# Loading x one pair of steps ahead in a cross-attention kernel

## The chip, the core and the metric

The kernel runs on one core of a Trainium2 chip. The metric is the time of one execution on the device in microseconds (us), given as the median of several runs. The core has five engines with queues of their own, each executed in order: TensorE (PE, with its weight loads shown as PEld), VectorE (DVE), ScalarE (ACT), GpSimd (POOL) and SyncE (SP). Here SP issues every DMA. Engines wait for each other, and for DMAs, by semaphores.

## What is computed

Cross-attention with 8 heads of width 256, a residual and a layer norm, in float32. x is 16 x 256 x 256, the context is 16 x 77 x 192, the mask 16 x 77.

```
Q, K, V = x @ Wq, context @ Wk, context @ Wv        (per head)
attn = softmax(where(mask, Q K^T / sqrt(256), -inf))
out = (attn V) @ Wo + x
result = (out - mean) * rsqrt(var + 1e-5) * gamma + beta
```

## The kernel before

**Folded weights.** The first part, up to about 43 us, multiplies weights with each other: gA and gB hold Wk times Wq per head, uA and uB hold Wv times Wo. From then on a batch needs only: `a`, its context with gA and gB (`prepare_a`); scores, x against `a` (`scores`, L289); a softmax; `vw`, its context with uA and uB (`prepare_vw`); and softmax weights times `vw`, which is the attention output before the residual.

**Tiles.** A batch is 256 rows of x, two tiles t of 128 rows (QT = 2, NT = 32 in all). Four batches make a group g (GB = 4, GT = 8 tiles). Each group has two copies of x in SBUF. `xg` has the rows as they are, for the residual; it is loaded by `load_x`, and the output is made in place in it. `xT` is x in transposed blocks, for the scores; `load_xT` (L144) loads it with four DMAs of 128 KB for two batches, one for each quarter of the partitions, and `transpose_x` (L154) turns the 32 x 32 blocks in place, two VectorE instructions for two batches (a pair). The xT of groups 0 and 2 share a buffer, and so do those of groups 1 and 3.

**The loop.** A step b runs from -1 to 14 (L937). In step b the scores of batch b+1 are made and its softmax follows, the product of batch b is made, and batch b-1 is normalised. For b below 13 (NS) the product of a batch is `seven(b)` (L434), seven block products in place of eight. It takes as weights the turned softmax `pT` and four sums of them, `ss`, which GpSimd makes in `sums(b)` (L415 to L418) in the step before. Its seven results are put together by `add_seven(b)`: two adds on VectorE (`add_product`, L483), two adds into m and three adds into `xg` on GpSimd (L469). The last batches use `attend` (L367) in its place.

The steps with odd b, up to b = 9, are long: TensorE also prepares two batches' `vw` and `a` there. The even ones are short. From b = 11 on (`alone`), each step prepares for one batch.

**Order within a step** (the order of the calls is the order on every queue: the schedule is written by hand). VectorE: shifts of the scores (L306, with the mask's `bias`), what the step before left in `behind`, statistics and `rden`, one `normalise` (L533, L552), two turns of softmax weights (L355), then `turn_x_and_normalise`, then `add_seven`'s adds. GpSimd: the softmax weights p (L345), `differences` (L398), then `sums` before `add_seven` in the odd steps up to 9, and `add_seven` before `sums` in the others. After `normalise` of the second tile of a pair, SP stores both (L560). `behind` holds the even steps' second `normalise`; it runs in the next step after the shifts, and so its store stands on SP ahead of that odd step's loads.

**Loads of x.** Group 0: xT in the first queue of loads, x by `load_x(0)` at L854. The other groups, in each odd step: x and xT for two batches that lie b+5 and b+6.

```python
        g, n = (b + 1) // GB + 1, (b + 1) % GB
        if g < NG and n % 2 == 0:
            load_x(g, n, 2 * QT)
            load_xT(g, n * QT, (n + 2) * QT)
```

They are turned one odd step later (batches b+3 and b+4), in `turn_x_and_normalise`, and their scores come in the steps b+2 and b+3.

**Masks.** `load_bias(lo, hi)` broadcasts the masks of some batches to all partitions; `bias_of(lo, hi)` makes them into what the shift adds (L569 to L574). Both are called for batches 0 to 3 and for 4 to 15; the later part is loaded at the end of the first queue of loads and made in step -1.

Of the kernel before, what the change touches and what calls it, by code (L numbers as in the profile page):

```python
# [10 lines left out]
I32 = mybir.dt.int32  # L11
# [5 lines left out]
P = 128  # L17
# [3 lines left out]
GB = 4  # L21
# [6 lines left out]
def kernel(  # L28
# [13 lines left out]
    nc = tc.nc  # L42
    B, S, DI = x.shape
    S2, DL = c.shape[1], c.shape[2]
    LB = DL - P
    CR = 112
    NG = B // GB
    QT = S // P
    NT = B * QT
    GT = GB * QT  # L50
# [48 lines left out]
    bias_f = bias.rearrange("p b k -> p (b k)")  # L99
# [14 lines left out]
    def load_x(g, n=None, of=QT):  # L114
        if not n:
            xg_of[g] = const.tile([P, GT, DI], F32, tag=f"xg{g}", name=f"xg_{g}")
        lo, hi = (0, GT) if n is None else (n * QT, n * QT + of)
        nc.sync.dma_start(xg_of[g][:, lo:hi], x_rows[:, g * GT + lo : g * GT + hi, :])
# [3 lines left out]
    def evacuate(dst, src):  # L122
# [3 lines left out]
        else:  # L126
            nc.vector.tensor_copy(dst, src)


    pools = {}  # L130
    xT_of, a_of, vw_of, p_of, mv_of = {}, {}, {}, {}, {}

    def in_two(name, shape, g):
        return pools[g % 2].tile(shape, F32, tag=f"{name}{g % 2}", name=f"{name}_{g}", bufs=1)

    def load_xT(g, lo=0, hi=GT):


        if lo == 0:
            xT_of[g] = in_two("xT", [P, GT * NM, 2, BK], g)  # L140
        rows = x.rearrange("b s d -> (b s) d")[(g * GT + lo) * P : (g * GT + hi) * P, :]
        rows = rows.rearrange("(m r) (i n) -> i r m n", r=BK, i=NM)
        for i in range(NM):
            nc.sync.dma_start(  # L144
                xT_of[g][i * BK : (i + 1) * BK, lo * NM : hi * NM].rearrange(
                    "p m n q -> p m (n q)"
                ),
                rows[i],
            )

    def transpose_x(g, j):

        cols = xT_of[g][:, j * NM : (j + 2) * NM]
        nc.vector.transpose(cols, cols)  # L154
# [127 lines left out]
    def scores(t):  # L282
        g = t // GT
        j, bl = t % GT, (t // QT) % GB
        ps = [ps_mm.tile([P, 512], F32, tag="mm", name=f"ps_{t}_{a}") for a in range(2)]
        for m in range(NM):
            for dc in range(2):
                for i in range(NM):
                    nc.tensor.matmul(  # L289
                        ps[m // 2][i * BK : (i + 1) * BK, m % 2 * 2 * S2 : (m % 2 + 1) * 2 * S2],  # L290
                        xT_of[g][:, j * NM + m, dc],
                        flat(a_of[g][:, dc, bl, 2 * i : 2 * i + 2, :]),
                        start=(dc == 0),
                        stop=(dc == 1),
                    )
        ps_of[t] = ps
# [234 lines left out]
    def centre(t):  # L531
        y = xg_of[t // GT][:, t % GT, :]
        nc.vector.scalar_tensor_tensor(  # L533
            y, y, mv_of[t // GT][:, t % GT, 0:1], gam, ALU.subtract, ALU.mult
        )

    def store(t):
        nc.sync.dma_start(out_rows[:, t, :], xg_of[t // GT][:, t % GT, :])

    def normalise(t, aside=False, centred=False):  # L540

        g, j = t // GT, t % GT
        rstd, less = rstd_of.pop(t)
        y = xg_of[g][:, j, :]
        if aside:
            nc.scalar.activation(y, y, AF.Identity, bias=less, scale=rstd)
            nc.gpsimd.tensor_tensor(y, y, gam, ALU.mult)
            nc.gpsimd.tensor_tensor(y, y, bet, ALU.add)
        else:
            if not centred:  # L550
                centre(t)
            nc.vector.scalar_tensor_tensor(y, y, rstd, bet, ALU.mult, ALU.add)  # L552
        if t >= NT - 5 * QT:
            store(t)
            return
        done.append(t)
        if t ^ 1 in done:
            t |= 1
            j |= 1
            nc.sync.dma_start(  # L560
                out_rows[:, t + 1 - QT : t + 1, :], xg_of[g][:, j + 1 - QT : j + 1, :]
            )
# [15 lines left out]
    with tc.tile_pool(name="wonce", bufs=1) as wp:  # L578
# [59 lines left out]
            load_blocks(wvT[:, a], wv_blocks[a])  # L638
        for a in range(NF):
            nc.sync.dma_start(wo_of[a // 2][:, a % 2], wo_rows[a])  # L640
        mask_row = mask.rearrange("b k -> (b k)")

        def load_bias(lo, hi):
            nc.sync.dma_start(
                bias_f[:, lo * S2 : hi * S2].bitcast(I32),
                mask_row[lo * S2 : hi * S2].partition_broadcast(P),
            )

        load_xT(0, 0, GT // 2)
        load_bias(0, GB)  # L650
        load_rest()
        load_xT(0, GT // 2, GT)
        load_bias(GB, B)


        idle = ps_mm.tile([P, P], F32, tag="mm", name="idle")
# [169 lines left out]
        def a_of_pairs(*pairs):  # L826
            part_A, part_B, copies = prepare_a(0, pairs)
            part_A()
            part_B()
            for dst, src in copies():  # L830
                nc.scalar.copy(dst, src)
# [19 lines left out]
        for i in range(3):  # L851
            turn_v(i)
        a_of_pairs(2, 3)
        load_x(0)  # L854
        nc.sync.dma_start(gam, gamma.partition_broadcast(P))
        nc.sync.dma_start(bet, beta.partition_broadcast(P))
        turn_v(3)
# [66 lines left out]

    behind = []

    def turn_x_and_normalise(g, n, old):
        to_turn = (g, 0) if g < NG and n == 2 else (g - 1, GT // 2) if g > 1 and n == 0 else None
        if to_turn:
            for j in range(to_turn[1], to_turn[1] + GT // 2, 2):  # L930
                transpose_x(to_turn[0], j)
        if old:
            normalise(old[1])

    assert QT == 2
    last = NT - 1
    for b in range(-1, B - 1):  # L937
        old = range(max(b - 1, 0) * QT, b * QT)
        now = range(max(b, 0) * QT, (b + 1) * QT)
        new = range((b + 1) * QT, (b + 2) * QT)  # L940
        for t in new if b >= 0 else ():
            scores(t)
        if b == B - 2:
            for t in old:
                finish(t)
            spread(old[0], old[-1] + 1)
            invert(old[0], old[-1] + 1, aside=old)
            for t in old:
                normalise(t, aside=True)
        for t in new if b >= 0 else ():  # L950
            shift(t)
        while behind:
            behind.pop(0)()
        g, n = (b + 1) // GB + 1, (b + 1) % GB
        if g < NG and n % 2 == 0:
            load_x(g, n, 2 * QT)
            load_xT(g, n * QT, (n + 2) * QT)
        for m in range(0, 2) if b < 0 else range(b + 2, min(b + 3, B // 2)):
            turn_last(m)
        alone = b + 1 >= B - GB  # L960
        works = work_of(b + 1) if alone or n % 2 == 0 else []
        for part_A, _, _ in works:
            part_A()
        for _, part_B, _ in works:
            part_B()
        for i, t in enumerate(new if b >= 0 else ()):
            exponential(t)
            if old and b < B - 2:
                finish(old[i])
            weigh(t)  # L970
        ahead = works and not alone
        if old and b < B - 2 and not ahead:
            spread(old[0], old[-1] + 1)
        if ahead:
            copy_out(works)
            if old:
                spread(old[0], old[-1] + 1)
            works = work_of(b + 2, rest_first=True)
            for _, part_B, _ in works:
                part_B()  # L980
            for part_A, _, _ in works:
                part_A()
        copy_out(works)
        if b + 1 < NS:
            differences(b + 1)
        if b < NS:
            if now:
                seven(b)
            if old:
                invert(old[0], old[-1] + 1)  # L990
                normalise(old[0])
            for t in new:
                turn(t)
            if b < 0:
                for j in range(GT // 2, GT, 2):
                    transpose_x(0, j)
                bias_of(GB, B)
            if alone or ahead:
                turn_x_and_normalise(g, n, old)
            else:  # L1000
                behind.append(partial(turn_x_and_normalise, g, n, old))
            if ahead:
                sums(b + 1)
            if now:
                add_seven(b)
            if b + 1 < NS and not ahead:
                sums(b + 1)
            continue
        for t in now:
            attend(t)  # L1010
        if b < B - 2:
            invert(old[0], old[-1] + 1, aside=old[:1])
            normalise(old[0], aside=True)
            turn(new[0])
            normalise(old[1])
            turn(new[1])
            for t in now:
                add_product(t)
        else:
            turn(new[0])  # L1020
            finish(now[0])
            spread(now[0], now[1])
            turn(new[1])
# [57 lines left out]
```

## Time and profile before

| | |
|---|---|
| median of 3 runs | 272.82 us (272.69 to 273.63) |
| the profiled execution | 272.17 us |
| its span in the profile | 270.3 us |
| TensorE busy | 263.6 us, 98% of the span |
| GpSimd busy | 171.4 us, 63% |
| VectorE busy | 185.6 us, 69% |
| ScalarE busy | 155.6 us, 58% |
| DMA | 22.69 MB, mean 84 GB/s |
| start of step 3 / 5 / 7 / 9 / 11 / 12 on TensorE (first scores) | 104.94 / 132.82 / 160.70 / 188.58 / 213.42 / 226.01 us |

Times in views are microseconds from the span's start. In a timeline a row is: start, length, engine, line, operation, output<-input, count, and in brackets how long the engine stood idle before it and what ended this. "The chain" is the work that ended last, followed back from the last instruction, at each step to what released it. Instructions of an engine can overlap a little, so a row's end can lie behind the next row's start.

### The profile page before, as it was taken

The page shows a single profiled execution, that of the slowest core. Times are in us where ns is not written, and L with a number is a line of the kernel's source. Part 1 is how long each engine was busy: PE and PEld are TensorE (multiplying, and loading weights), DVE is VectorE, ACT ScalarE, POOL GpSimd, SP SyncE. Part 2 cuts the span into 40 slices and gives each one's busy share as a digit, 9 for nine tenths or more (in the row PEclk, how much of TensorE's full clock was granted, in tenths as well). Part 3 has the DMA queues.
Part 4 walks back from the last instruction along what each step waited for, and adds up shares of the span by engine and source line. Part 5 has one row for each costly group of instructions (what it writes and reads, how often), then busy time and mean ns, then how long its engine had stood idle before and what let it go on. Part 6 is the DMA issues. An engine that isn't in the chain of part 4 may idle for free.

```text
span 270.3 us, 14362 instructions
## 1 busy us (share of the span) xinstructions
PE 263.6 (98%) x6104; PEld 190.5 (70%) x6104; DVE 185.6 (69%) x808; ACT 155.6 (58%) x652; POOL 171.4 (63%) x231
## 2 busy tenths in 40 slices
PE   7999999999999999999999999999999999999993
PEld 6557588754894599449954996489769969684662
DVE  0555938583464858863796479646977898988765
ACT  3233325835858555964687377729584592945752
POOL 1000005726389757996699759964999798966654
PEclk9999999999999999999999999999999999999999
DMA  6998999993000010261016100910091010110102
GB/s 194 203 202 187 327 173 164 309 191 52 2 5 5 2 42 5 75 125 44 2 51 151 41 6 7 191 45 4 7 189 51 2 45 4 44 41 2 62 22 81
DMA packets 42512, 22.69 MB, mean 84 GB/s; under 512 B 23680, under 2 KB 41680, under 8 KB 42448
## 3 DMA queue, kind: packets, MB, share of 16 engines
q1 hardware_dynamic: 42448, 21.77, 37.3%
q8 instruction: 48, 0.79, 1.3%
q14 instruction: 16, 0.13, 0.2%
HBM read 17.57 MB, written 4.19 MB: 81 GB/s over the span
## 4 chain that ended last, share of the span: by engine, by line
PE 91%; DMA 5%; SPq 2%; DVE 1%; issue 0%; DVEq 0%
PE ps L289 25%; PE pa L180 11%; PE pv L214 11%; PE po L434 10%; PE pm L434 9%; PE pv L225 6%; PE pa L192 5%; DMA wk_blk<-in_L_xattn_Wk_dram 5%; PE po L367 4%; PE pu L737 3%; PE pr L248 2%; PE pgb L797 1%; PE pw L751 1%; PE pr L260 1%; SPq L596 1%; PE po L383 1%
## 5 line engine op out<-in xcount | busy, mean ns | idle before, releaser
L324 ACT ACTIVATE e<-s,top 128x77 f32<-128x77 f32 x256 | 83.8, 346 | 46.6 <-DVE top L306 42.6
L289 PE MATMUL ps<-a,xT 128*32 128x154 f32 x2048 | 69.9, 294 | 0.0
L289 PEld LDWEIGHTS ps<-a,xT 128*32 128x32 f32 x2048 | 66.2, 110 | 1.2 <-ACT uB L886 0.4
L345 POOL TENSOR_TENSOR p<-e,rden 128x512 f32<-128x512 f32 x64 | 47.7, 772 | 24.1 <-DVE rden L339 24.1
L306 DVE CUSTOM_DVE_ANT_0 s<-ps,bias 128x77 f32<-128x77 f32 x256 | 43.5, 232 | 15.3 <-PE ps L289 15.3
L324 ACT ACTIVATION_READ_ACCUMULATOR e<-s,top 128x1 f32 x208 | 38.9, 187 | 0.0
L180 PE MATMUL pa<-cA,gA 128*32 128x308 f32 (+1 forms) x576 | 36.4, 394 | 0.0
L469 POOL TENSOR_TENSOR xg<-xg,m 128x256 f32<-128x256 f32 x39 | 28.7, 737 | 7.8 <-DVE xg L483 5.8
L180 PEld LDWEIGHTS pa<-cA,gA 128*32 128x32 f32 x576 | 18.4, 110 | 20.2 <-issue 7.0
L214 PE MATMUL pv<-uA,cA 128*32 128x512 f32 x256 | 30.6, 595 | 0.0
L552 DVE SCALAR_TENSOR_TENSOR xg<-xg,rstd,bet 128x256 f32<-128x256 f32 x26 | 21.2, 816 | 12.8 <-ACT rstd L513 11.5
L398 POOL TENSOR_TENSOR ts<-vw 128x768 f32<-128x768 f32 x13 | 24.0, 1849 | 7.9 <-ACT vw L923 7.9
L355 DVE STREAM_TRANSPOSE pT<-p 128x640 f32<-128x640 f32 x32 | 25.7, 822 | 3.2 <-POOL p L345 3.1
L923 ACT COPY vw<-pv 128x512 f32<-128x512 f32 x32 | 17.7, 584 | 14.7 <-PE pv L214 7.7
L306 DVE DVE_READ_ACCUMULATOR2_ANT top<- 128x1 f32 x256 | 20.8, 81 | 0.0
L483 DVE TENSOR_TENSOR xg<-po,xg 128x256 f32<-128x256 f32 x31 | 11.6, 407 | 13.4 <-PE po L434 12.4
L192 PE MATMUL pa<-cB,gB 64*32 64x308 f32 (+1 forms) x576 | 20.3, 392 | 0.0
L572 POOL TENSOR_TENSOR nan<-nan 128x4 f32<-128x4 f32 (+1 forms) x2 | 0.4, 203 | 31.0 <-DVE nan L571 31.0
L923 ACT COPY a<-pa 128x308 f32<-128x308 f32 (+1 forms) x56 | 18.9, 399 | 1.7 <-PE pa L180 0.2
L192 PEld LDWEIGHTS pa<-cB,gB 64*32 64x32 f32 x576 | 10.7, 107 | 12.3 <-issue 7.5
L225 PE MATMUL pv<-uB,cB 64*32 64x512 f32 x256 | 17.3, 597 | 0.0
L533 DVE SCALAR_TENSOR_TENSOR xg<-xg,mv,gam 128x256 f32<-128x256 f32 x27 | 16.7, 619 | 0.1
(118 smaller groups left out, 409.4 us busy)
## 6 DMA issues: line engine op xcount, KB each, us to landing
xT<-in_x_dram SPq DMA_DIRECT2D x32, 128.0 KB, 5.8
xg<-in_x_dram SPq DMA_DIRECT2D x6, 512.0 KB, 5.0
out_dram<-xg SPq DMA_DIRECT2D x11, 256.0 KB, 2.5
wo<-in_L_xattn_Wo_dram SPq DMA_DIRECT2D x4, 512.0 KB, 6.0
wq_blk<-in_L_xattn_Wq_dram SPq DMA_DIRECT2D x12, 128.0 KB, 4.5
wvT<-in_L_xattn_Wv_dram SPq DMA_DIRECT2D x16, 96.0 KB, 3.4
out_dram<-xg SPq DMA_DIRECT2D x10, 128.0 KB, 2.0
wk_blk<-in_L_xattn_Wk_dram SPq DMA_DIRECT2D x12, 96.0 KB, 4.4
```

The costliest lines, as they stand in the source:

```text
L180: nc.tensor.matmul(flat(o[i * BK : (i + 1) * BK]), gA[:, h, cols(dc, i)], flat(cA[:, batches, :]), start=not rest_first and n in opening, ...
L192: nc.tensor.matmul(flat(banks[j + k][i * BK : (i + 1) * BK]), gB[half(k), h // 2, cols(dc, i)], flat(cB[half(k), batches, :]), start=rest_ ...
L214: nc.tensor.matmul(pv[k][i * BK : (i + 1) * BK], cA[:, b, k * BK : (k + 1) * BK], uA[:, parts, :, i], start=not rest_first, stop=rest_first,)
L225: nc.tensor.matmul(pv[k][i * BK : (i + 1) * BK], cB[half(k), b, k * BK : (k + 1) * BK], uB[half(k), parts, :, i], start=rest_first, stop=n ...
L289: nc.tensor.matmul(ps[m // 2][i * BK : (i + 1) * BK, m % 2 * 2 * S2 : (m % 2 + 1) * 2 * S2], xT_of[g][:, j * NM + m, dc], flat(a_of[g][:, ...
L306: nc.vector.tensor_tensor_reduce(s[:, h], ps[a][:, k * S2 : (k + 1) * S2], bias[:, b, :], scale=-1.0, scalar=FAR, op0=ALU.add, op1=ALU.min ...
L324: nc.scalar.activation(e[:, h], s[:, h], AF.Exp, bias=top[:, one], scale=-1.0, accum_out=den[:, one] if t < QT * NS else None,)
L345: nc.gpsimd.tensor_tensor(part, e_mh[:, :, :, keys], rden_mh.unsqueeze(3).to_broadcast(list(part.shape)), ALU.mult,)
L355: nc.vector.transpose(pT_of[t].rearrange("p n m q -> p m n q"), p.rearrange("p m (n k) -> p m n k", k=BK),)
L434: nc.tensor.matmul(out[i * BK : (i + 1) * BK], weight[:, i], moving, start=first and n == 0, stop=final and n == len(terms) - 1,)
L469: nc.gpsimd.tensor_tensor(to, to, what, ALU.add)
L923: nc.scalar.copy(dst, src)
```

## The change

- `load_bias` of the masks of batches 4 to 15 moves from the end of the first queue of loads to step -1, in front of that step's loads.
- x of group 0 is loaded in two: batches 0 and 1 where all four were loaded, batches 2 and 3 in step -1.
- In each odd step b, x and xT of batches b+3 and b+4 are loaded, where it was b+5 and b+6 (in step -1 only x, since xT of group 0 is loaded at the start). The last such loads stand in step 11.
- The turn of xT stays in the odd step that it was in (batches b+3 and b+4), which is now the step of its load, and it goes behind the second `normalise` of that step in place of ahead of it.

```diff
-        load_xT(0, GT // 2, GT)
-        load_bias(GB, B)
+        load_xT(0, GT // 2, GT)
...
-        load_x(0)
+        load_x(0, 0, 2 * QT)
...
-    def turn_x_and_normalise(g, n, old):
-        to_turn = (g, 0) if g < NG and n == 2 else (g - 1, GT // 2) if g > 1 and n == 0 else None
-        if to_turn:
-            for j in range(to_turn[1], to_turn[1] + GT // 2, 2):
-                transpose_x(to_turn[0], j)
+    def normalise_and_turn_x(b, old):
         if old:
             normalise(old[1])
+        coming = (b + 3) * QT
+        if b > 0 and b % 2 and coming < NT:
+            for j in range(coming % GT, coming % GT + 2 * QT, 2):
+                transpose_x(coming // GT, j)
...
-        if g < NG and n % 2 == 0:
-            load_x(g, n, 2 * QT)
-            load_xT(g, n * QT, (n + 2) * QT)
+        if b < 0:
+            load_bias(GB, B)
+        coming = (b + 3) * QT
+        if b % 2 and coming < NT:
+            load_x(coming // GT, coming % GT // QT, 2 * QT)
+            if b > 0:
+                load_xT(coming // GT, coming % GT, coming % GT + 2 * QT)
```

In the changed kernel the lines from L130 on are shifted by some lines; the prediction names lines of the kernel before.

More of the change, by code (lines that the diff above doesn't have):

```diff
@@ L127, in evacuate, with load_bias @@
             nc.vector.tensor_copy(dst, src)
+    mask_row = mask.rearrange("b k -> (b k)")
+    def load_bias(lo, hi):
+        nc.sync.dma_start(
+            bias_f[:, lo * S2 : hi * S2].bitcast(I32),
+            mask_row[lo * S2 : hi * S2].partition_broadcast(P),
+        )
     pools = {}
@@ L640 @@
             nc.sync.dma_start(wo_of[a // 2][:, a % 2], wo_rows[a])
[L641 to L647, printed above, removed]
         load_xT(0, 0, GT // 2)
@@ L998 @@
             if alone or ahead:
-                turn_x_and_normalise(g, n, old)
+                normalise_and_turn_x(b, old)
             else:
-                behind.append(partial(turn_x_and_normalise, g, n, old))
+                behind.append(partial(normalise_and_turn_x, b, old))
             if ahead:
```

## The prediction

> **What bounds the kernel now.** I read the page first: busy shares, the granted clock, and the chain that ended last.
>
> ```profile
> PE 263.6 (98%) x6104; PEld 190.5 (70%) x6104; DVE 185.6 (69%) x808; ACT 155.6 (58%) x652; POOL 171.4 (63%) x231
> PEclk9999999999999999999999999999999999999999
> ...
> PE 91%; DMA 5%; SPq 2%; DVE 1%; issue 0%; DVEq 0%
> ```
>
> TensorE is busy for 98% of the span at full clock, and the chain is TensorE for 91%. The chain in order of time says it more sharply: up to 20.31 us it goes through weight loads and a transposed weight, from 20.31 to 265.73 us it is matmul after matmul with no gap, and the last 4.6 us are VectorE's. The waits of PE agree: two, 1.4 and 0.4 us, both in the first part. So an edit that adds no matmul and moves only DMAs and VectorE work can lengthen the run by making TensorE wait once, and can shorten it only ahead of 20.31 us. The question is therefore where TensorE's slack against VectorE, GpSimd and the loads is smallest.
>
> **The early part (masks, first half of x).** In the built program's order TensorE, ScalarE, VectorE and GpSimd issue as many instructions as before; SP has one issue more, since x's first load is split. The late masks' issue moves from 43.88 to behind `bet` (issued 46.20, 0.74 us). All moved issues stood at 43.88 us or later, so none was ahead of the chain's DMAs (last one landed by 19.30): gain nothing. Cost: the masks' load, issued at about 47 and landing at most 7.4 us later (the slower of the two mask rows), is there by 54.4; its reader on VectorE (L569) starts at 61.75. Cover 7.3 us; without it that reader, and the `shift` of batch 4 behind it, would be late. The x and xT loads of batches 4 and 5 move from step -1 to step 1, but step 1 has no store ahead of it on SP's queue, so they are issued straight behind those of step -1. The same ten issues ended at 59.9 us before, and their first reader is the turn at 92.11: nothing. The new waits that the pool's other order of tiles brings name weight loads and the L751 matmuls, all past by 43.7 us: nothing.
>
> **The later loads, and who waits for them.** From step 3 on, a pair's x and xT are issued in the odd step that turns them. There they stand on SP behind the store of an earlier pair, as the older loads did; those rows give the interval from that store's issue to the last landing. This is step 3 on SP, start and length first, the last line from a narrower window:
>
> ```profile
> 111.76 0.40 SPq L560 DMA_DIRECT2D out_dram<-xg  x1
> 112.21 0.46 SPq L118 DMA_DIRECT2D xg<-in_x_dram  x1
> ```
>
> ```profile
> 114.38 0.82 SPq L144 DMA_DIRECT2D xT<-in_x_dram  x1
> ```
>
> The list of DMA issues for that window gives this last piece's time to landing:
>
> ```profile
> xT<-in_x_dram SPq DMA_DIRECT2D x1, 128.0 KB, 6.7
> ```
>
> So 114.38 + 6.7 = 121.1, 9.3 us after the store's issue. The same reading gives 7.9 in step 5 (143.33 + 4.2 - 139.63), 8.8 in step 7 (170.54 + 6.2 - 167.91) and 8.7 in step 9 (199.13 + 5.7 - 196.10).
>
> The turn (L154, two transposes, 1.26 us) now goes behind `normalise` of the older tile and waits for that landing; behind it on VectorE stand the two L483 adds, then the next step's shifts. In steps 3, 5 and 7 the turn began at 118.87, 146.75 and 174.62; with a centring and scaling first (about 1 us) it would begin at 119.9, 147.8 and 175.6, and waits 1.2, 0 and 1.1 us. VectorE then idled 3.4, 3.4 and 3.1 us for TensorE before the L483 adds, so the wait is hidden there. In step 9 the turn waits from 203.5 to 204.8 and ends at 206.1 instead of 205.4; GpSimd needs the L483 result only at 207.30, behind its sums and the two adds into m, and the shifts, some 0.3 us late, catch up in their three 0.33 us idle gaps: hidden too. The prices if this cover were gone are part of the slow rival.
>
> Step 11 has no such cover. VectorE there, in the timeline:
>
> ```profile
> 225.87 0.84 DVE L355 STREAM_TRANSPOSE pT<-p 128x640 f32<-128x640 f32 x1 [0.49 <-POOL p L345]
> 226.64 1.26 DVE L154 STREAM_TRANSPOSE xT<-xT 128x512 f32<-128x512 f32 x2
> 227.83 0.50 DVE L533 SCALAR_TENSOR_TENSOR xg<-xg,mv,gam 128x256 f32<-128x256 f32 x1
> 228.37 0.56 DVE L552 SCALAR_TENSOR_TENSOR xg<-xg,rstd,bet 128x256 f32<-128x256 f32 x1
> 228.85 0.74 DVE L483 TENSOR_TENSOR xg<-po,xg 128x256 f32<-128x256 f32 x2
> ```
>
> VectorE runs without a pause, and GpSimd (next view) waited 0.69 us for L483 and then makes, in order, three adds into x and the four sums `ss` of batch 12:
>
> ```profile
> 229.34 2.36 POOL L469 TENSOR_TENSOR xg<-xg,m 128x256 f32<-128x256 f32 x3 [0.69 <-DVE xg L483]
> 231.66 0.74 POOL L415 TENSOR_TENSOR ss<-pT 128x256 f32<-128x256 f32 x1
> 232.34 0.75 POOL L416 TENSOR_TENSOR ss<-pT,pT 128x256 f32<-128x256 f32 x1
> 233.17 0.74 POOL L417 TENSOR_TENSOR ss<-pT,ss 128x256 f32<-128x256 f32 x1
> ```
>
> TensorE loads these sums as weights in step 12, right behind the first product (`pm` L434):
>
> ```profile
> 234.82 0.46 PEld L434 LDWEIGHTS pm<-vw,ss 128*32 128x32 f32 x16
> ```
>
> L417 ends at 233.91: the slack of the whole chain L483, L469, ss, pm is 234.82 - 233.91 = 0.91 us. The other sums were added ahead of the adds into x in the odd steps 3 to 9; only step 11 has this order.
>
> The store ahead of the new load of step 11 stays where it is:
>
> ```profile
> 220.65 0.40 SPq L560 DMA_DIRECT2D out_dram<-xg  x1
> ```
>
> Then xT has landed at 220.65 + 8.75 (between the two middle intervals) = 229.4. VectorE is free for the turn earlier: from 226.64 the L533 and L552 pair takes 1.02 us as here, or 1.79 as at 218.72 beside GpSimd, so 227.7 to 228.4. The landing decides. The next instruction starts 1.19 us after a pair of transposes begins (226.64 to 227.83), so L483 starts at 229.4 + 1.19 = 230.59 instead of 228.85: 1.74 us later. GpSimd, which was waiting for it, passes it on, L417 ends at 235.65, and TensorE waits 1.74 - 0.91 = **0.83 us**. From both sides: the shortest interval, 7.9, gives landing 228.55 and L483 0.89 later, inside the slack, stall 0; the longest, 9.3, gives 229.95, L483 2.29 later, stall 1.4. I take the middle. Nothing below nothing: no matmul goes away.
>
> What is late next: the bank that L483 empties is wanted by the second `pa` bank of step 12 at about 232.0, and L483 ends at 231.3 (231.9 in the long case), so no wait. VectorE's and GpSimd's later work, delayed up to 2 us, next meets TensorE at the products of batch 13, L367 at 245.51, whose second transposed p stood ready at 238.7: cover 6.8 us. Every later matmul moves by the stall, and so does the end.
>
> **A rule against the trace.** The four xT pieces of these steps took 4.2 to 6.7 us to land. The Trainium skill, DMA: Bandwidth & Descriptors, section "Anatomy of one DMA", gives a fit of about 2 us plus bytes over 436 GB/s for a transfer from the gpsimd path; an estimate from it is 2.3 us for a 128 KB piece, which would land by 225.6 in step 11, ahead of the turn, and the sum would be 272.8. Its section "Rules for kernel authors" says to issue a DMA early and wait on it late, which speaks against this change. The row decides here, since five transfers run together.
>
> **The sum.** The profiled execution took 272.17 us (span 270.3, 1.87 outside it); with 0.83 it would be 273.0. The median of the runs, 272.82, lies 0.65 above; the same step gives 273.65. I predict **273.6 us**.
>
> **Rivals.**
> - The load is in time and TensorE does not wait: 272.8. For it: step 5 landed in 7.9, and everything up to 228.57 in step 11 is free. Against it: three of four intervals were 8.7 or more. That the loads are not really issued late has the same price; the order on SP shows them behind the stores, except for step 1.
> - Slower by more: the same wait in step 11, but long. The stall is the landing minus 228.57, so from a landing at 229.93 (9.28 after the store, about the longest of four) it exceeds 1.36 us. Some xT pieces of the early part took 8.9 us; a last piece issued at 223.3 (220.65 + 170.54 - 167.91) would land at 232.2, stall 3.6, time 276.4. For it: the 9.3 of step 3. Against it: that 8.9 was under the weight loads' traffic.
> - Faster: less traffic early lets the weights land sooner. The price can only lie ahead of 20.31 us, where no moved issue stands; nothing in the profile speaks for it.
>
> **How the numbers follow.** Half a per cent, 1.36 us, is about what a measurement here can tell from no change. Stall in step 11 within 1.36 us: 0.51. No stall: 0.24. Longer stall: 0.22. Faster: 0.03. So faster 0.03, same 0.75, slower 0.22. The range runs from 272.4 (no stall, and the runs' own scatter: 272.17 profiled, 272.69 lowest) to 275.0 (the long bound's 1.4, 274.2, and part of the slow rival).
>
> **What would show it.** On SP, xT issues of step 11 behind the store at about 220.7. On VectorE, an idle stretch of 1 to 2 us in front of L154's line in step 11, ended by DMA xT, and shorter ones in steps 3, 7 and 9. On the chain, a first GpSimd piece between 234 and 237 us and TensorE waiting for ss there, and no wait anywhere else. It is wrong if TensorE waits for a turn or a mask, or in steps 3 to 9, or if VectorE's wait ends after 230.

## The result, and the profile after

| | before | after |
|---|---|---|
| median | 272.75 us (22 runs) | 273.89 us (22 runs) |
| ratio, 95% interval | | 1.0041 [1.0025, 1.0056] |
| the profiled execution, its span | 272.17, 270.3 us | 273.85, 272.1 us |
| first scores (L289, after L297) to the last product, on TensorE | 43.62 to 265.28: 221.66 us | 43.87 to 266.95: 223.08 us |

The changed kernel is 1.14 us slower by the medians. The ratio leaves out one of the 22 runs of after, which took 709.87 us; the longest of the others took 275.52. The last row is a yardstick for all that follows: it leaves out the first part, whose length differs between executions (by 0.25 us here), and counts what TensorE loses after it. After loses 1.42 us there. In the views of the changed kernel and of those made from it, lines of the helpers are 8 higher than before (L289 is now L297, L483 is L491, L434 is L442); "busy VectorE alone" keeps the lines of before.

The page of after, the lines that answer to those of before:

```profile
PE 264.5 (97%) x6104; PEld 191.7 (70%) x6104; DVE 187.2 (69%) x808; ACT 155.5 (57%) x652; POOL 172.0 (63%) x231
PEclk9999999999999999999999999999999999999999
...
PE 90%; DMA 5%; SPq 2%; DVE 1%; issue 1%; DVEq 0%
```

The same work at the same clock. One share of the chain is new: "issue 1%", time in which an engine waited for nothing that the profile shows. The waits of PE in after say which line it stands ahead of (us in total, times, longest; a third wait, of 0.2 us, is left out here):

```profile
PE idle L659 <- POOL ident masks.py:199: 1.4, 1, 1.4
PE ps L297 <- issue: 1.1, 1, 1.1
```

The first stands at the start of the program, as before. Where the second lies is told by the chain of after in order of time (start, length, what):

```profile
224.12 2.17 PE po L442 x64
226.29 0.37 PE ps L297 x9
226.66 1.07 issue
227.73 4.00 PE ps L297 x116
231.73 0.12 PE pv L222
```

TensorE stops behind the ninth score matmul of step 12, and from there on its work is late: the next scores start 13.97 us later (226.29 to 240.26), where before took 12.58 for the same work. That is 1.39 of the 1.42 us. (From the start of one matmul to that of the next it is 1.36 us, where 0.03 is usual; the row's 1.07 leaves out the modelled end of the last matmul.) The loss is in the step that the prediction named, but neither at the place in it nor for the reason that it gave.

The predicted chain is there as well. SP of after in step 11, then VectorE and GpSimd:

```profile
221.15 0.40 SPq L568 DMA_DIRECT2D out_dram<-xg  x1
221.60 0.46 SPq L118 DMA_DIRECT2D xg<-in_x_dram  x1
222.11 2.40 SPq L152 DMA_DIRECT2D xT<-in_x_dram  x4
```

```profile
227.14 1.25 DVE L541 SCALAR_TENSOR_TENSOR xg<-xg,mv,gam 128x256 f32<-128x256 f32 x1
228.42 0.56 DVE L560 SCALAR_TENSOR_TENSOR xg<-xg,rstd,bet 128x256 f32<-128x256 f32 x1
230.09 1.31 DVE L162 STREAM_TRANSPOSE xT<-xT 128x512 f32<-128x512 f32 x2 [1.10 <-DMA xT<-in_x_dram]
231.32 0.72 DVE L491 TENSOR_TENSOR xg<-po,xg 128x256 f32<-128x256 f32 x2
```

```profile
231.78 2.35 POOL L477 TENSOR_TENSOR xg<-xg,m 128x256 f32<-128x256 f32 x3 [2.48 <-DVE xg L491]
234.09 0.73 POOL L423 TENSOR_TENSOR ss<-pT 128x256 f32<-128x256 f32 x1
234.78 0.73 POOL L424 TENSOR_TENSOR ss<-pT,pT 128x256 f32<-128x256 f32 x1
235.59 0.73 POOL L425 TENSOR_TENSOR ss<-pT,ss 128x256 f32<-128x256 f32 x1
```

The loads stand behind the store, VectorE waits 1.10 us for xT, GpSimd 2.48 for VectorE, and the third sum is ready at 235.59 + 0.73 = 236.32. TensorE's weight load of these sums in after:

```profile
236.48 0.46 PEld L442 LDWEIGHTS pm<-vw,ss 128*32 128x32 f32 x16
```

It starts 0.16 us after the sum is there and shows no wait. But TensorE had been put back 1.33 us by then (1.36 less the usual 0.03); without the pause it would have wanted the sums at about 235.15 (236.48 - 1.33) and waited about 1.2 us for them. This assumes that nothing else would have moved. So two delays end in one place, each about as long as the whole loss, and the profile of one execution cannot tell which of them is needed.

### The profile page after: what moved, and what is told of

It reads as the page before. It is cut to its first block, busy times and chain, and to the rows that moved or that the text cites. A ratio compares the mean times of both kernels' runs of the same rounds, so it can differ in the third digit from the quotient of the medians.

```text
span 272.1 us, 14365 instructions
## 1 busy us (share of the span) xinstructions
PE 264.5 (97%) x6104; PEld 191.7 (70%) x6104; DVE 187.2 (69%) x808; ACT 155.5 (57%) x652; POOL 172.0 (63%) x231
## 4 chain that ended last, share of the span: by engine, by line
PE 90%; DMA 5%; SPq 2%; DVE 1%; issue 1%; DVEq 0%
PE ps L297 25%; PE pa L188 11%; PE pv L222 10%; PE po L442 10%; PE pm L442 8%; PE pv L233 6%; PE pa L200 5%; DMA wk_blk<-in_L_xattn_Wk_dram 5%; PE po L375 4%; PE pu L736 3%; PE pr L256 2%; PE pgb L796 1%; PE pw L750 1%; PE pr L268 1%; PE po L391 1%; SPq L604 1%
## 5 line engine op out<-in xcount | busy, mean ns | idle before, releaser
L297 PE MATMUL ps<-a,xT 128*32 128x154 f32 x2048 | 70.3, 294 | 1.1 <-issue 1.1
L297 PEld LDWEIGHTS ps<-a,xT 128*32 128x32 f32 x2048 | 66.4, 110 | 2.4 <-issue 1.3
L491 DVE TENSOR_TENSOR xg<-po,xg 128x256 f32<-128x256 f32 x31 | 11.5, 405 | 11.7 <-PE po L442 10.7
L541 DVE SCALAR_TENSOR_TENSOR xg<-xg,mv,gam 128x256 f32<-128x256 f32 x27 | 18.2, 675 | 0.1
```

The costliest lines, as they stand in the source:

```text
L297: nc.tensor.matmul(ps[m // 2][i * BK : (i + 1) * BK, m % 2 * 2 * S2 : (m % 2 + 1) * 2 * S2], xT_of[g][:, j * NM + m, dc], flat(a_of[g][:, ...
```

## The experiments

**Theory V** is the prediction: VectorE's wait for xT in step 11 delays `ss`, and TensorE waits for it. **Theory C** is the rival that the pause suggests: TensorE waits for the next piece of its own program, which comes late while the loads of x are under way. The records of DMA give it a start: the queue of kind "instruction" moves 48 packets in this execution, and 6104 matmuls over 48 packets are on average 127 matmuls to a packet.

Ratios are against the kernel before, timed beside it on the same chip. "Loss" is the yardstick above, in the profiled execution, less before's 221.66.

| kernel | median us | ratio, 95% interval | loss us | TensorE in steps 9 to 12 |
|---|---|---|---|---|
| the change again | 274.08 | 1.0023 [0.9996, 1.0051] | 1.49 | pause behind 9th score, step 12 |
| early part alone | 272.85 | 0.9999 [0.9980, 1.0018] | 0.09 | nothing |
| turn last | 272.94 | 0.9997 [0.9979, 1.0015] | 0.08 | nothing |
| sums first | 273.50 | 1.0003 [0.9977, 1.0029] | 1.05 | same pause |
| turn last, sums first | 273.90 | 1.0030 [0.9998, 1.0062] | 1.12 | same pause |
| busy VectorE alone | 273.98 | 1.0028 [1.0001, 1.0056] | 1.79 | waits for ss |
| burst alone | 272.62 | 0.9991 [0.9967, 1.0015] | 0.70 | short pause, step 9 |
| last pair early | 274.44 | 1.0053 [1.0036, 1.0070] | 2.26 | pause in step 10 |
| the same, busy VectorE | 276.76 | 1.0132 [1.0115, 1.0149] | 3.61 | pause, waits for ss and xg |
| last pair in step 10 | 273.84 | 1.0015 [0.9988, 1.0042] | 0.96 | pause in step 10 |
| program 8 later | 275.22 | 1.0077 [1.0053, 1.0101] | 4.01 | pause behind 1st score, step 12 |
| program 32 later | 275.15 | 1.0076 [1.0054, 1.0098] | 0.52 | waits for ss |

**The change again.** No edit.

> The changed kernel as it is, for a second profile beside its relatives. Both theories expect 1.004. V expects TensorE to wait in step 12 either at pm for ss, or earlier by a pause that hides that wait; the weights of the second pm product start when L425 has ended. C alone expects the pause near 226.7 us again, and ss early enough.

The time is 0.99 us above before's median, the pause is 1.04 us long, behind the same ninth matmul, and the weights of `ss` start 0.06 us after the sum is ready. The pause is no accident of one execution.

**The early part alone** (kernel before, with masks and x of group 0 loaded as in the change, and nothing later).

```diff
-        load_bias(GB, B)
...
-        load_x(0)
+        load_x(0, 0, 2 * QT)
...
+        if b < 0:
+            load_bias(GB, B)
+            load_x(0, 2, 2 * QT)
```

> The kernel before with the early part of the change alone: x of group 0 loaded in two halves and the masks of the later batches loaded in step -1; x of the later groups is loaded and turned as before. Both theories: nothing, ratio 0.998 to 1.002, TensorE without a wait over 0.3 us from the first scores on. If the early part has a cost that the profile hid, the ratio is above 1.002.

0.9999, and a loss of 0.09 us. The early part costs nothing, as forecast.

**Turn last.** The changed kernel, with step 11's turn of xT behind the adds and sums on VectorE; all loads stay.

```diff
+        if b < B - 5:
+            turn_x(b)
...
+            if b == B - 5:
+                turn_x(b)
```

> The changed kernel, but in step 11 VectorE turns xT behind the two L483 adds of add_seven, so that nothing that GpSimd's sums wait for stands behind the load. The load's burst of 1 MB stays where it is. Theory V (the forecast: VectorE's wait for xT delays the sums ss of batch 12, and TensorE waits for them) expects the time of before, ratio 1.000 +- 0.001, about 272.8 us. Theory C (TensorE's instructions come late because the burst of x shares the DMA engines with their fetch: the pause of 1.07 us in the scores of step 12 that the changed kernel's profile shows) expects the loss to stay, ratio 1.004, with the pause near 226.7 us on TensorE.

0.9997: the loss is gone. VectorE still waits for xT (0.44 us), but now behind L491, which starts at 229.53. The chain of this kernel at the place where after's has its pause:

```profile
224.67 2.17 PE po L442 x64
226.85 4.19 PE ps L297 x128
231.03 1.72 PE pv L222 x16
```

128 scores in one piece. That speaks for V; but the pause is gone too, though the loads are unchanged. So this kernel alone cannot tell V from C.

**Sums first.** The changed kernel, with GpSimd making `ss` ahead of its adds in step 11, as it does in the long steps before.

```diff
-            if ahead:
+            first = ahead or b == B - 5
+            if first:
                 sums(b + 1)
...
-            if b + 1 < NS and not ahead:
+            if b + 1 < NS and not first:
```

> The changed kernel, with loads, turn and VectorE's order as they are; only on GpSimd the four sums of batch 12 come ahead of add_seven in step 11. VectorE still waits for xT. V (the path goes L483, adds into x, sums) expects ratio 1.000 to 1.001. C expects 1.004.

1.0003, the median 0.41 us above before's. The third sum is ready at 230.55 (229.82 + 0.73), more than 5 us ahead of its weight load (236.08), so nothing of V is left; yet the profiled execution has the pause again, 0.74 us behind the ninth score.

**Both of these.** The two edits together.

> The changed kernel with both earlier remedies in step 11: VectorE turns x behind the product that GpSimd waits for, and GpSimd makes its sums ahead of the additions. No trace is left of VectorE's wait in GpSimd's sums; the loads of x are as in the changed kernel. Theory V: the loss is gone, ratio 0.998 to 1.001. Theory C as the main cause: a pause of about 1 us in the scores of step 12 remains and costs its length, ratio 1.003 to 1.005; with a pause in some executions only, 1.000 to 1.002.

1.0030 with an interval from 0.9998 to 1.0062: unclear between the theories by time. The profile is clear: a pause of 0.81 us at the same place and a loss of 1.12 us, with V excluded twice over. In a profiled execution the pause alone can cost a microsecond.

**Busy VectorE alone.** V without C: the kernel before, with four more transposes of an xT that nobody reads again, in step 11 ahead of L483.

```diff
+        if g == NG and n == 0:
+            for j in range(0, GT, 2):
+                transpose_x(NG - 2, j)
```

> The kernel before, and in step 11 VectorE makes four more transposes in place (xT of group 2, read no more) behind the turn and ahead of the L483 adds: about 2.5 us of VectorE, no load moved, no burst. V expects L483 2.5 us later and TensorE waiting for ss at pm in step 12: 2.5 - 0.9 = 1.6 us, ratio 1.006 (a wait at pa for the bank that L483 empties may come first and is then part of it). C expects 1.000.

1.0028, the median 0.89 us above. The chain of this kernel, where it leaves VectorE:

```profile
227.35 3.63 DVE xT L154 x6
230.98 0.38 DVE xg L533
231.36 0.02 issue
231.38 0.48 DVE xg L552
231.87 0.34 DVE xg L483
...
236.10 0.73 POOL ss L417
236.83 0.04 issue
236.88 1.52 PE pm L434 x48
```

And the weight load that waits, in the timeline of PEld:

```profile
236.88 0.38 PEld L434 LDWEIGHTS pm<-vw,ss 128*32 128x32 f32 x16 [1.32 <-POOL ss L417]
```

This is the predicted mechanism, link by link, with no pause in it: in VectorE's timeline L483 starts at 231.78 where before had 228.85, 2.93 us later, and TensorE waits 1.32 us. (Some 0.5 of the loss of 1.79 us lies elsewhere, at 51 to 62 us.)

**Burst alone.** The kernel before, with 1 MB more loaded in step 11, as much as in the change but all of it in blocked pieces of 128 KB, into an xT that nobody reads again; its own loads stay where they were.

```diff
+        if b == B - 5:
+            for m in range(0, GT, 2 * QT):
+                reload_xT(NG - 2, m, m + 2 * QT)
```

> The kernel before, and in step 11, at the place where the changed kernel issues its last loads, eight more DMAs of 128 KB each from x into the xT of group 2, which is read no more: the burst without anyone who waits for it. V expects 1.000. C expects a pause of about 1 us on TensorE, ended by nothing that the profile shows, in step 11 or 12: ratio 1.003 to 1.004.

0.9991, no pause in steps 11 and 12. A 1 MB burst there need not cost anything. (The one pause, 0.33 us in step 9's products, falls beside loads that the kernel before has as well; so such a pause is not peculiar to the change.)

**Last pair early.** The changed kernel, with the loads of step 11 moved into step 9, which so has 2 MB.

```diff
-        if b % 2 and coming < NT:
...
+        for coming in (coming, coming + 2 * QT)[: 2 if b == B - 7 else 1]:
+            if b % 2 and coming < NT and b != B - 5:
...
```

> The changed kernel, but x and xT of batches 14 and 15 are loaded in step 9, right behind those of batches 12 and 13; the turn stays in step 11 and finds its data there. Both V and C expect the loss of step 11 to go, ratio 1.000 +- 0.001 (C allows a new pause in step 9 or 10, where the burst is now 2 MB). If the loss were in steps 3 to 9 or in the early part, it would stay: 1.004.

1.0053, no better than the change (their intervals overlap), though no VectorE instruction of step 11 waits for a load any more: 1.000 was expected of both theories, with a new pause allowed for C. The chain of this kernel:

```profile
205.33 3.66 PE ps L297 x112
209.00 1.80 issue
210.79 0.73 PE ps L297 x16
```

The pause came with the loads into the scores of step 10.

**The same with a busy VectorE** (four more transposes in step 11, ahead of the turn).

> As e2_last_pair_early, and in step 11 VectorE makes four more transposes, in place on the xT of group 2, which is read no more, ahead of the turn: some 2.5 us of VectorE in the place where the changed kernel waited for the load, without the burst. V expects L483 about 2.5 us later, TensorE waiting 2.5 - 0.9 = 1.6 us for ss at pm in step 12, ratio 1.005 to 1.006. C expects 1.000.

1.0132, 0.0079 above the kernel without them, 2.2 us. The pause is at the same matmul (0.98 us this time), and the added VectorE work makes TensorE wait 1.0 us for `ss` and 0.9 for `xg`. Here the two delays meet TensorE in different steps, and the cost of the second comes on top of the first.

**Last pair in step 10**, with no other load beside it.

```diff
-        if b % 2 and coming < NT:
+        if b == B - 6:
+            coming += QT
+        if (b % 2 and b != B - 5 or b == B - 6) and coming < NT:
```

> The changed kernel, but x and xT of batches 14 and 15 are loaded in step 10, 1 MB in each of steps 9, 10; the turn stays in step 11 and finds its data there. V expects 1.000. If the loss of e2_last_pair_early came from the doubled burst in step 9 (its profile shows a pause of 1.8 us on TensorE at 209.0), that goes as well: 1.000; if it came from something else in the change, it stays at 1.005.

1.0015, unclear; a pause of 0.52 us at 213.38, again beside the loads. No better than the kernel before.

**The program 8 matmuls later.** The changed kernel, with twelve small transposes in place of four large ones at the very start of TensorE's program.

```diff
-        keep_busy(12)
+        keep_busy(8)
+        for i in range(12):
+            nc.tensor.transpose(idle[:BK, :BK], ident[:BK, :BK], ident[:BK, :BK])
```

> The changed kernel, with four of the twelve large transposes of the identity that open TensorE's program replaced by twelve small ones (32x32): every later matmul stands 8 places further on in TensorE's program, and nothing else moves; the four cost about 0.24 us each and the twelve small ones are estimated at about 0.06 each from the matmuls of 32 columns, so the start should move by under 0.5 us. Theory C (the pause of 1.07 us in the scores of step 12 is TensorE waiting for the next piece of its program): the pause moves 8 matmuls forward, from behind the ninth score matmul of that step to behind the first. Theory V alone (the delay of VectorE is all, and the pause is some wait that belongs to this matmul's data): the pause stays behind the ninth, or is not there and TensorE waits 0.8 to 1.3 us for ss. Time by both: ratio 1.002 to 1.005.

The chain of this kernel:

```profile
226.99 2.17 PE po L442 x64
229.17 0.11 PE ps L297
229.28 1.88 issue
231.16 4.26 PE ps L297 x124
```

The pause moved from behind the ninth score to behind the first. Counted from the start of the program it stands behind the 5161st matmul in both kernels: it belongs to the place in the program, not to the matmul or its data. The time, 1.0077, missed the expected range of 1.002 to 1.005. The profiled execution, 277.54 us, was the longest of the seven: in it the first part ran 1.1 us longer than in after, the pause is 0.8 longer, and TensorE lost 1.6 us between 48 and 54 us, 0.7 of it a wait for VectorE. What the shift itself adds to the median was not tried.

**The program 32 matmuls later** (`keep_busy(4)` and forty small ones).

> The changed kernel, with eight of the twelve large transposes at the start of TensorE's program replaced by forty small ones (32x32): every later matmul stands 32 places further on. Theory C: the pause leaves the scores of step 12; the piece is now wanted behind about the forty-first of the last 64 products of step 11, some 1.1 us sooner against the loads of x, and was asked for sooner as well; so a pause of 0 to 1.1 us there or none, and what it no longer covers is seen as a wait of TensorE for ss at the first GpSimd piece of step 12 (0.2 to 1.2 us). Theory V alone: wait for ss of 0.8 to 1.3 us or the same pause behind the ninth score matmul. Time by both: ratio 1.001 to 1.005, with up to 1 us either way from the start, which can be read off where the scores of step 1 begin.

No pause at all, and what it had covered comes to light. The chain of this kernel:

```profile
231.06 1.30 DVE xT L162 x2
232.37 0.64 DVE xg L491 x2
...
236.58 0.74 POOL ss L425
237.33 0.04 issue
237.37 1.52 PE pm L442 x48
```

and the load of weights at its end:

```profile
237.37 0.38 PEld L442 LDWEIGHTS pm<-vw,ss 128*32 128x32 f32 x16 [0.40 <-POOL ss L425]
```

This is the predicted chain in the changed kernel itself. The wait is only 0.40 us here: the turn of xT starts 231.06 - 222.77 = 8.3 us after the store's issue, where in after it was 230.09 - 221.15 = 8.9. The total of 1.0076 is no measure of it: the first scores start 1.95 us later than before's (45.57), and that was put in by the forty transposes or by this execution's loads of weights. The loss after that is 0.52 us.

**What follows.** V is shown by two kernels, with its chain (busy VectorE alone; program 32 later). C's pause is shown to belong to a place in the program: in the profiles it stands behind matmul 4529 (burst alone), 4656 (last pair early, with and without the busy VectorE), 4783 (last pair in step 10) and 5161 (five profiles), and 4656 - 4529 and 4783 - 4656 are 127, 5161 - 4783 is 3 x 126: the spacing of the instruction packets.

The records of the packets agree. In after, the views of DMA from 225 us on and from 225.5 us on say of their queue (packets, MB, share):

```profile
q8 instruction: 9, 0.15, 1.3%
q8 instruction: 8, 0.13, 1.2%
```

So the 40th of the 48 packets began between these two moments; its record runs from 225.21 to 226.13, and it had begun ahead of the pause (226.66 to 227.73). In before its record is 222.72 to 224.13. In all nine profiles with such a pause, TensorE went on 1.3 to 1.7 us after one packet had ended: the 35th, 36th, 37th or 40th, for the matmuls 4529, 4656, 4783 and 5161 in this order. In the six profiles without loads of x in step 11 the 40th packet ended 2.0 to 2.5 us before the 5161st matmul started; in the eight with them it ended between 2.3 us before and 0.5 us after that. The two kernels with the change's loads and no pause are those where it came in good time: turn last 1.7 us before, program 32 later 2.3. That the loads delay the packet is the reading that fits, but no run varied the packet alone, and why it is sometimes late and sometimes not stays open.

Which of the two sets the median of after can be told only roughly. Weighted by their intervals, the kernels without V (turn last, sums first, both) are at 1.0004 and the two measurements of the change at 1.0037, each within about 0.0014: taking V away gives back most of the loss, an estimated 0.9 of 1.0 us. But two of those three show a loss of 1.1 us, nearly all of it from the pause, in their profiled execution. How often the pause comes in executions that are not profiled stays open.

No kernel here is faster than the one before.

## Why the prediction was right, and where it was not

**The bound, and the early part: right.** TensorE still sets the end; the early part alone measures 0.9999.

**The loads behind the store: right.** Forecast for step 11: the landing 8.75 us after the store's issue, between 7.9 and 9.3. Read in the same way (issue of the last piece and its time to landing), after has 223.77 + 6.2 - 221.15 = 8.8, and the kernels with the program moved or with both edits 8.2 to 9.2. In steps 3 and 9 the waits were forecast to end at 121.1 and 204.8; the turns started at 121.35 and 205.06, and it cost nothing. In step 7 no wait came where 1.1 us was forecast: the last piece landed 8.1 us after the store's issue, not 8.8.

A rule was weighed there: the fit in the Trainium skill, DMA: Bandwidth & Descriptors, section "Anatomy of one DMA", is given for one transfer of the gpsimd path, and the estimate from it for a 128 KB piece was 2.3 us. The four pieces of step 11, issued by SP one behind the other, took a median of 6.3, so the rows of before were the right guide, as chosen.

**VectorE and GpSimd in step 11: right in kind, 0.7 us short in size.** L491 was forecast at 230.59 and came at 231.32; the sum was forecast at 235.65 and came at 236.32. Of the 0.7, the store's issue accounts for 0.5 (221.15 for 220.65; 0.28 of it is the whole steady part starting later), the time from there to the turn's start for 0.19 (8.94 for 8.75). The prediction called itself wrong if VectorE's wait ended after 230; the piece landed at 229.97 and the turn started at 230.09, so this sign was met, by a tenth of a microsecond, where the whole steady part was 0.28 late.

**TensorE's stall: the size is near, in part by luck, and the place is not as forecast.** The step that failed is "TensorE waiting for ss there, and no wait anywhere else". In after's profile TensorE does not wait for `ss`; it pauses 9.5 us earlier, at the place in its program where a late instruction packet belongs, and 1.33 us are lost where 0.83 was forecast. Left to itself the wait for `ss` would have been about 1.2 (above), also more than 0.83, by the 0.7 of the step before less what the whole steady part was late (0.28). The working never looked at what TensorE's own instructions need of the DMA engines: the profile of before has no such pause, and no row warned of it. That the time lies so near the forecast is luck as far as this profile goes: a delay that was not foreseen covered the one that was, and is about as long.

**The sum.** Forecast 273.0 for the profiled execution, which took 273.85: 0.28 more in start, 0.56 more lost in the scores' stretch (1.39 against 0.83). Forecast 273.6 for the median, which is 273.89, a little inside the half per cent that was called no change. **The rivals:** no stall (272.8) is near what "turn last" gives (272.94); the long wait did not come; nor did anything faster.

## What to carry to other kernels

When a load is moved to just ahead of its use, follow the wait past the engine that has it: here VectorE's wait of 1.1 us can reach TensorE by way of GpSimd, because step 11, unlike the odd steps before it, has GpSimd's sums behind its adds, and so behind VectorE. Two delays that end in one place hide each other; take away each alone and both before saying which one costs. And a pause that the profile puts down to "issue" can be tested by moving the program a few instructions: if the pause stays at its count, it belongs to the program and not to the data. The records of the instruction queue then say whether a packet came late.

## What the runs showed of the hardware

- TensorE pauses of 0.3 to 1.9 us, put down to "issue", beside loads of x. They stand 126 to 127 matmuls apart or a multiple (4529, 4656, 4783, 5161), in a program of 6104 matmuls with 48 instruction packets, and each ended 1.3 to 1.7 us after the packet of that place had arrived. The profile of before shows none; that of burst alone shows one of 0.33 us beside loads that before has as well.
- The same VectorE instruction (the first scaling of `normalise` in step 11, 128x256) took 0.50 us in before beside GpSimd's two adds of 128x128 into m, and 1.25 us in after beside its `differences` of 128x768 (226.30 to 228.07). It cost nothing here, since the landing came later still.
